# A graph network's first 112 nodes taken out of the count matrix and summed by gathers

## The chip, the cores and the metric

The kernel runs on one core of a Trainium2 chip. The core's engines each run their own stream of instructions and wait for each other through semaphores: TensorE (PE in the profile, its weight loads PEld), VectorE (DVE), ScalarE (ACT), GpSimd (POOL) and SyncE (SP), which only issues DMAs. ACT and POOL issue DMAs too. The metric is the time of one execution on the device, in microseconds (us).

## The reference

There are N = 2500 nodes with 256 features and E = 80000 directed edges, sorted by destination (about 32 edges a node). Cut to what matters:

```python
h = relu(layernorm(x))
xs = [h]
for W, b in ((W0, b0), (W1, b1), (W2, b2)):          # three layers
    xi, xj = h[dst], h[src]
    m = concatenate([xi, xj - xi], -1) @ W + b        # W is 512 x 256
    s = segment_sum(m, dst, N)                        # sum over the edges of each node
    h = relu(s / max(cnt, 1))                         # cnt: edges of each node
    xs.append(h)
out = x + concatenate(xs, -1) @ Wf + bf
```

Since the sum is linear, with W split into Wt (top half) and Wb, the sum for node n is cnt[n] * h[n] @ (Wt - Wb) + (sum over its edges of h[src] @ Wb) + cnt[n] * b. The middle term is a product with the count matrix A, where A[m, n] is the number of edges from node m to node n.

## The kernel before

**Layout.** Nodes stand in NT = 20 tiles of 128 (NP = 2560 rows). `hT` holds the features transposed, 256 features x NP nodes. `zh` and `zl` hold z = h @ Wb for all nodes, as a rounded part and the remainder, so that two fast matmuls (float32r) give nearly float32 accuracy. `acc` gathers the output, one tile of 128 nodes x 256 at a time. Row PAD of the last tile of `zh`, `zl` holds the bias, and row PAD of the count matrix holds `cnt`, so that the bias enters by the same product.

**Count matrix.** Destinations are taken in windows of W = 6 nodes: 417 windows, whose edges are fetched by indirect DMA (`get_edges`, L542), one window to a partition, in WG = 4 rounds of 128 windows, at most CAP = 256 edges each. `compare` (L755, VectorE) makes one-hot matrices of four windows, `counts` (L773, PE) multiplies them, `take_counts` (L782, ACT) writes the result to the tile `a`. Windows are put together in NG = 5 groups of columns: four of 84 windows (504 columns) and one of 81 (486 columns). A finished group is given its row of counts by `finish` (L800, on POOL) and stored to DRAM (`a_dram`), since only two groups fit in SBUF; layers 1 and 2 load three groups each (`load_a`, L806).

**A layer.** `layer` (L817) makes one group of columns: for each of the 20 node tiles and both halves of the features, one matmul with `zh` and one with `zl` as weights and the group of `a` as the moving operand (80 matmuls, L832), then four float32 matmuls with `wt` and `hT` (eight instructions on PE, L836), then a ReLU on ACT that overwrites the group's columns of `hT` (L839). Before a layer's groups, `nodes_split` (L708) makes `zh` and `zl` from `hT` tile by tile (L711, L720, L721). `final` (L731) adds a tile's product with its part of Wf to `acc` (L734, L736) before the tile of `hT` is overwritten.

**Order.** The stage before layer 0 follows a list written out by hand (L864): normalisation (N), transposes (T, R), products (Z, H, L for z, F, G for the output), edge search and the counting of group 0 (B, C, E). Layer 0 makes group g while the counts of group g + 1 are built between its matmuls; most of its instructions are recorded through a helper that keeps them in program order, so they all carry line L280. Layers 1 and 2 run the groups up or down, so that the two groups left in SBUF come first. In layer 1 `add_x` (L724) brings x and the last bias to `acc`: 20 DMAs on POOL's queue and 40 additions on POOL. After layer 2 the last 20 `final` calls store the output.

**Queues.** SP issues the loads of inputs and weights and the stores and loads of `a`; POOL issues the indirect DMAs and those of `add_x`. Each queue issues in order: an instruction that waits holds back all behind it.

Of the kernel before, what the change touches and what calls it, by code (L numbers as in the profile page):

```python
# [280 lines left out]
        return ordered  # L281


DONE = object()


def run(it):
    for _ in it:
        pass
# [22 lines left out]
def by_windows(ctx: ExitStack, tc: tile.TileContext, x, src, dst, Ws, bs, Wf, bf, out, missing):  # L312
# [13 lines left out]
    CH = 2  # L326
    S = 8
    CAP = CH * P
    NW = (N + W - 1) // W
    NV = NW * W  # L330
    WG = (NW + P - 1) // P
    NB = NT * W
    BW = 4
    TURN = 3
# [1 line left out]
    AHEAD = 4  # L336
    GWS = []
    while sum(GWS) < NW:
        GWS.append(min(84, NW - sum(GWS)))
    G = max(GWS) * W  # L340
    GS = 512
    NG = len(GWS)
    Q = NT // 2
    assert NT == 2 * Q
# [2 lines left out]
    MORE = 4 - R % 4  # L347
    HR = (R + MORE) // 2
    assert NP <= 4096 and HR <= 512
    assert E == P * R and NV <= NP and BW * NB <= 512 and G <= 512 and CAP <= 256  # L350
    assert E + P < 2 ** 24 and NV - (NT - 1) * P <= PAD < P and D == DC * P

    const = ctx.enter_context(tc.tile_pool(name="const", bufs=1))
    dram = ctx.enter_context(tc.tile_pool(name="wdram", bufs=1, space=DRAM))
# [32 lines left out]
    lim = const.tile([P, WG], F32, name="lim")  # L387

    const.tile([P, 24], F32, name="between")
    a_dram = [dram.tile([P, NT, G], F32, name=f"a_dram{g}") for g in range(NG)]  # L390

    apools = [ctx.enter_context(tc.tile_pool(name="apool0", bufs=1))]
# [40 lines left out]
    load_wt(0, SPo)  # L433

    lim_i = pp.tile([P, WG], I32, name="lim_i")
    POOLo.iota(lim_i, pattern=[[P * W, WG]], base=0, channel_multiplier=W)
    limr_i = pp.tile([P, WG * P], I32, name="limr_i")
    POOLo.iota(limr_i, pattern=[[W, WG * P]], base=0, channel_multiplier=0)
    row_i = pp.tile([P, MORE], I32, name="row_i")
    POOLo.iota(row_i, pattern=[[0, MORE]], base=-P, channel_multiplier=1)  # L440
    make_identity(nc, ident)
# [10 lines left out]
    load_b(1)  # L452
    DVE.memset(ones, 1.0)
    DVE.memset(ones_b, 1.0)
    DVE.memset(cnt[:, NV:], 0.0)
    POOL.tensor_copy(ident_b, ident)
    warm = pp.tile([P, 1], F32, name="warm")
    ACTo.activation(warm, ones, AF.Sqrt)
    idle = pp.tile([P, 512], BF16, name="idle")
# [94 lines left out]
    def key_parts(i):  # L554
# [3 lines left out]
        DVEo.tensor_scalar(away[:, i, :], ed, lim[:, i:i + 1], -1.0, op0=OP.subtract, op1=OP.max)  # L558
        parts[i] = [lo_i]

    def key_low(i):
        km = pw.tile([P, CAP], F32, name="km")
        ACTo.copy(km, parts[i][0])
        parts[i][0] = km

    def key_high(i):

        hi_i = edges[i][0]
        DVEo.tensor_scalar(hi_i, hi_i, ~(P - 1), 4, op0=OP.bitwise_and, op1=OP.logical_shift_right)
        kn = pw.tile([P, CAP], F32, name="kn")  # L570
        DVEo.scalar_tensor_tensor(kn, away[:, i, :], float(W), hi_i, op0=OP.min, op1=OP.add)
        parts[i].append(kn)
# [15 lines left out]
    def degrees(i):  # L588

        for q in range(W + 2):  # L590
            junk = hot.tile([P, CAP], BF16, name="junk2")
            ACTo.activation(junk, away[:, i, :], AF.Relu, bias=nc_[:, q:q + 1], accum_out=gsum[:, i, q:q + 1])
            yield
        DVEo.scalar_tensor_tensor(deg[:, i, :], gsum[:, i, 1:W + 1], -2.0, gsum[:, i, 0:W], op0=OP.mult, op1=OP.add)
        DVEo.tensor_add(deg[:, i, :], deg[:, i, :], gsum[:, i, 2:W + 2])
        DVEo.tensor_copy(deg_b[:, i, :], deg[:, i, :])
        yield
        yield
        yield
        yield  # L600
        for w0 in range(0, min(P, NW - i * P), P // 2):
            n = min(P // 2, NW - i * P - w0)
            pc = bank()
            for c in range(W):
                PEo.matmul(pc[:, :n * W].rearrange("p (w c) -> p w c", c=W)[:, :, c],
                          deg_b[:, i, c:c + 1].to_broadcast([P, P]), ident_b[:, w0:w0 + n], start=True, stop=True)
            ACTo.copy(cnt[:, (i * P + w0) * W:(i * P + w0 + n) * W], pc[:, :n * W])
            yield

    def shares():  # L610
        cnt_n = bank()
        for t in range(NT):
            PEo.matmul(cnt_n[:, t:t + 1], cnt[0:1, t * P:(t + 1) * P], ones_b, start=True, stop=True)
        found = hot.tile([P, 1], F32, name="found")
        DVEo.reduce_sum(found, deg.rearrange("p i c -> p (i c)"), axis=mybir.AxisListType.X)
        pf = bank()
        PEo.matmul(pf[0:1, 0:1], found, ones, start=True, stop=True)
        DVEo.tensor_scalar(missing, pf[0:1, 0:1], float(E), None, op0=OP.not_equal)
        yield
        some = hot.tile([P, NT], F32, name="some")  # L620
        DVEo.tensor_scalar(share, cnt_n[:, :NT], 1.0, None, op0=OP.max)
        DVEo.reciprocal(share, share)
        DVEo.tensor_scalar(some, cnt_n[:, :NT], 1.0, None, op0=OP.min)
        DVEo.tensor_mul(share, share, some)
        yield
# [95 lines left out]
            DVE.scalar_tensor_tensor(zl[:, t, :], pz[:, :D], sc, zh[:, t, :].bitcast(F32),  # L721
                                     op0=OP.mult, op1=OP.subtract)

    def add_x(t):  # L724
        n = P if t < NT - 1 else LAST
        xb = hot.tile([P, D], F32, name="zf")
        POOL.dma_start(xb[:n], x[t * P:t * P + n, :])
        POOL.tensor_add(xb[:n], xb[:n], bf_sb[:n])
        POOL.tensor_add(acc[:n, t, :], acc[:n, t, :], xb[:n])

    def final(l, t):  # L731
        po = bank()
# [7 lines left out]


    def group_of(g):
        return sum(GWS[:g]) * W, GWS[g] * W

    def touched(g):
        c0, n = group_of(g)
# [52 lines left out]

    def finish(g, a):  # L800
        c0, n = group_of(g)
        POOLo.tensor_copy(a[PAD:PAD + 1, NT - 1, :n], cnt[PAD:PAD + 1, c0:c0 + n])
        SP.dma_start(a_dram[g][:, :, :n], a[:, :, :n].bitcast(F32))
        yield

# [4 lines left out]
        return a  # L810

    def by_count(g):
        c0, n = group_of(g)
        for o in range(DC):
            DVEo.tensor_mul(hT[:, o, c0:c0 + n], hT[:, o, c0:c0 + n], cnt[:, c0:c0 + n])

    def layer(l, g, a, own, PE=PE, ACT=ACT):  # L817

# [27 lines left out]

    groups = [(0, 1), (1, 2), (2, 4), (4, 6), (6, 8), (8, Q)]
    a = new_a(0)
    acts = {
        "lim": limits, "first": find_first, "next": find_next, "pick": find_rows,  # L850
        "dstr": lambda: ACTo.copy(dst_r[:, MORE:], dst_i),
        "pk": lambda i: pick_half(i // 10, i % 10), "sg": lambda i: count_half(i // 10, i % 10),
        "se": lambda i: search(*((0, 1), (1, WG))[i]), "ge": get_edges,
        "ka": key_parts, "km": key_low, "kb": key_high, "kt": key_turn,
        "k1": lambda i: key_copy(i, 0), "k2": lambda i: key_copy(i, 1),
        "io": small_numbers, "ws": lambda: DVEo.tensor_sub(ws[0][0], ws[0][0], ws[0][1]),
        "st": stats, "rs": lambda g: spread(*groups[g]), "sq": lambda g: roots(*groups[g]),
        "sc": lambda g: scales(*groups[g]), "N": normalize, "T": turn, "R": take_turned,
        "Z": lambda q: product(q, ws[0][1]), "V": lambda q: with_b(), "H": split_high, "L": split_low,
        "F": lambda q: product(q, wfs[0]), "G": first_final,  # L860
        "B": compare, "C": counts, "E": lambda b: take_counts(b, a),
        "warm": keep_warm,
    }
# [3 lines left out]
        sc3 L0 sg21 N6 pk31 ka0 kb0 Z1 N5 st8 N7 G1 T6 rs5 sg10 sg31 km0 T5 se1 kt0 R6 H1 st2 F6 sq5 sc5 k10 k20  # L867
        rs2 Z6 ge1 L1 T7 B0 R5 R7 Z5 B1 C0 B2 ka1 G6 H6 N9 H5 C1 T9 F7 E0 ge2 kb1 R9 sq2 km1 E1 kt1 C2 B3 k21 Z9
        k11 N8 L6 B4 E2 L5 C3 B5 C4 T8 E3 E4 C5 V9 R8 E5 ge3 ka2 H9 sc2 Z7 H7 F8 G7 B6 N3 N2 ka3 km2 T2 R2 km3
        kb2 C6 T3 kb3 B7 L7 kt2 Z2 B8 B9 L9 E6 C7 k22 k12 kt3 H2 N4 E7 B10 k13 k23 Z8 L2 C8 T4 C9 E8 C10 H8 E9  # L870
        F9 B11 B12 C11 G8 E10 C12 R4 E12 E11 B13 F5 B14 C13 R3 B15 C14 E13 E14 L8 B16 Z3 G9 B17 C15 C16 H3 E15
        G5 B18 F3 C17 E16 C18 F4 E17 B19 C19 Z4 L3 G3 B20 E18 C20 B21 F2 E19 B22 E20 H4 L4 G4 B23 B24 G2 ws
    """

    def perform(order):
# [20 lines left out]

    held = None
    LATE = [NT] * 4
    extra = chain(degrees(0), finish(0, a), later_loads(), degrees(1))
    for g in range(NG):  # L900
        at = {}
        own = LATE
        if g + 1 < NG:
            a1 = new_a(g + 1)
            one = build(g + 1, a1)
            left = -(-len([b for b in windows if b[0] == g + 1]) // TURN)
            units = NT + DC * DC
            at = {(i + 1) * (units - 1) // left - 1 for i in range(left)}
            if g:
                own = [u + 1 - i for i, u in enumerate(sorted(at)[1:5])]  # L910
        else:
            extra = shares()
        for u, _ in enumerate(layer(0, g, a, own, PEo, ACTo)):
            if u in at:
                next(one)
            next(extra, None)
            if g == 0 and u % 2:
                next(extra, None)
            if g == 0 and u == NT // 2 + 3:
                by_count(0)  # L920
            if u == NT - 1 and g + 1 < NG:
                run(extra)
                by_count(g + 1)
        run(extra)
        if g + 1 < NG:
            run(finish(g + 1, a1))
            held, a = a, a1
        extra = chain(degrees(g + 2) if g + 2 < WG else ())
    DVEo.tensor_sub(ws[1][0], ws[1][0], ws[1][1])
    tiles = {NG - 1: a, NG - 2: held}  # L930
    for l in range(1, L):
# [1 line left out]
        if l % 2:  # L933
            groups.reverse()

        last = touched(groups[0])
        for t in [t for t in range(NT) if t not in last] + last:
            nodes_split(l, t)
        if l + 1 < L:
            load_b(l + 1)  # L940
            load_wb(l + 1)
# [2 lines left out]
        for j, g in enumerate(groups):  # L944
            for t in touched(g):
                if t not in finished:
                    finished.add(t)
                    final(l, t)
                    if l == 1:
                        add_x(t)  # L950
            if j == NG - 1:
                load_wf(l + 1)
            run(layer(l, g, tiles[g], LATE))
# [2 lines left out]
            if j + 2 < NG:  # L956
                del tiles[g]
                tiles[groups[j + 2]] = load_a(groups[j + 2])

    for t in [*range(NT - 3), NT - 1, NT - 3, NT - 2]:  # L960
        final(L, t)
# [38 lines left out]
```

## Time and profile before

| What | Value |
|---|---|
| Median of 3 runs | 517.1 us (517.03 to 517.1) |
| The profiled execution's own time | 517.24 us |
| Its span, first to last instruction | 515.4 us |
| Granted TensorE clock | 0.999 of full speed |
| Stage before layer 0 | to 62.3 us |
| Layer 0 (counts built inside) | 62.3 to 210.5 us |
| Layer 1 | 210.5 to 352.0 us |
| Layer 2 | 352.0 to 493.3 us |
| Last stage | 493.3 to 515.4 us |
| One group's load or store of `a` | 5040 KB, 17.2 to 17.3 us from issue to landing |

The stages are read from the chain that ended last: the work followed back from the last instruction, at each step to what released it. "Busy" is the time in which an engine had an instruction under way; matmuls overlap, so the cost of one is the distance from start to start, which is the length of a piece of the chain over the number of instructions in it. A float32 matmul is two instructions on PE.

### The profile page before, as it was taken

The numbers are of one execution on the slowest core, as the hardware profiler recorded it, in microseconds if no ns is written. First come the engines' busy times: TensorE is split into PE (matmuls) and PEld (weight loads), VectorE is DVE, ScalarE is ACT, GpSimd is POOL, SyncE is SP. The second block draws the span as 40 slices with busy tenths as digits, with TensorE's granted clock in tenths as the row PEclk, the third lists the DMA queues.
The fourth block names the chain that finished last, engine by engine and source line by source line (L and its number), as shares of the span: only waits on it lengthen the run. The fifth ranks groups of instructions, "written<-read, shape, count | busy, mean of one in ns | idle before, by whom it ended". The sixth has DMA issues, their size and how long they took to land.

```text
span 515.4 us, 6981 instructions
## 1 busy us (share of the span) xinstructions
PE 508.1 (99%) x2864; PEld 407.2 (79%) x2864; DVE 213.5 (41%) x455; ACT 134.1 (26%) x307; POOL 68.5 (13%) x103
## 2 busy tenths in 40 slices
PE   8999999999999999999999999999999999999996
PEld 4898888778778788788787878787887878787875
DVE  7989998889888840360101010103501010101033
ACT  5776666644534320330000000004300000000000
POOL 2680000000000000017241424200000000000000
PEclk9999999999999999999999999999999999999999
DMA  9110008950906428011576665100005565730023
GB/s 277 50 43 0 1 2 325 336 215 15 378 11 232 171 80 318 22 31 48 180 261 207 236 229 214 32 1 1 1 0 197 205 219 183 252 136 20 1 84 121
DMA packets 38111, 68.74 MB, mean 133 GB/s; under 512 B 1201, under 2 KB 37065, under 8 KB 38071
## 3 DMA queue, kind: packets, MB, share of 16 engines
q1 hardware_dynamic: 35798, 63.49, 34.8%
q0 software_dynamic: 1344, 3.61, 2.3%
q10 hardware_dynamic: 928, 1.11, 0.7%
q8 instruction: 24, 0.39, 0.3%
q14 instruction: 17, 0.13, 0.1%
HBM read 40.03 MB, written 28.18 MB: 132 GB/s over the span
## 4 chain that ended last, share of the span: by engine, by line
PE 90%; DVE 4%; DMA 3%; POOL 2%; issue 1%; SPq 0%; DVEq 0%
PE pa L832 35%; PE pa L280 21%; PE bank L734 10%; PE bank L280 8%; PE bank L711 7%; PE pa L836 7%; PE pz L280 2%; DMA acc<-in_x_dram 2%; POOL acc L280 1%; DVE one_m L280 1%; DVE st L280 1%; DMA es<-in_src_dram,start_i 1%; POOL ed L280 1%; DVE one_n L280 1%; POOL es L280 0%
## 5 line engine op out<-in xcount | busy, mean ns | idle before, releaser
L832 PE MATMUL pa<-a,zh 128*128 128x504 f32 (+1 forms) x400 | 156.4, 391 | 0.0
L832 PE MATMUL pa<-a,zl 128*128 128x504 f32 (+1 forms) x400 | 154.5, 386 | 0.0
L736 DVE SCALAR_TENSOR_TENSOR acc<-bank,share,acc 128x256 f32<-128x256 f32 x60 | 29.0, 484 | 213.6 <-PE bank L734 213.5
L832 PEld LDWEIGHTS pa<-a,zh 128*128 128x128 f32 x400 | 75.2, 188 | 14.9
L832 PEld LDWEIGHTS pa<-a,zl 128*128 128x128 f32 x400 | 75.1, 188 | 14.8
L280 PE MATMUL pa<-a,zh 128*128 128x504 f32 (+1 forms) x200 | 84.0, 420 | 0.0
L280 DVE TENSOR_TENSOR one_m<-iota_m,key_m 128x1024 bf16<-128x1024 bf16 (+1 forms) x105 | 72.1, 687 | 15.2 <-PE bank L280 15.1
L280 PE MATMUL pa<-a,zl 128*128 128x504 f32 (+1 forms) x200 | 77.7, 389 | 0.0
L839 ACT ACTIVATE hT<-pa 128x1008 f32<-128x1008 f32 (+1 forms) x10 | 10.1, 1005 | 238.8 <-PE pa L836 238.8
L280 ACT CAST a<-bank 128x480 fp32r<-128x480 f32 (+1 forms) x105 | 52.9, 565 | 68.5 <-PE bank L280 65.9
L280 DVE TENSOR_TENSOR one_n<-iota_n,key_n 128x960 bf16<-128x960 bf16 (+1 forms) x105 | 69.7, 664 | 0.0
L734 PE MATMUL bank<-wf,hT 128*128 128x256 f32 x240 | 53.6, 379 | 0.0
L734 PEld LDWEIGHTS bank<-wf,hT 128*128 128x128 f32 x240 | 45.6, 190 | 9.8 <-issue 4.1
L280 PEld LDWEIGHTS <-one_m 128*128 128x128 bf16 x834 | 45.5, 98 | 9.8 <-issue 7.0
L280 PE MATMUL bank<-one_n,one_m 128*128 128x120 bf16 x834 | 51.4, 217 | 0.3
L280 PEld LDWEIGHTS pa<-a,zh 128*128 128x128 f32 x200 | 37.8, 189 | 10.3 <-issue 2.6
L280 PEld LDWEIGHTS pa<-a,zl 128*128 128x128 f32 x200 | 37.7, 189 | 8.9 <-issue 2.6
L721 DVE SCALAR_TENSOR_TENSOR zl<-bank,share,zh 128x256 fp32r<-128x256 f32 x38 | 18.4, 484 | 56.0 <-ACT zh L720 55.9
L836 PE MATMUL pa<-hT,wt 128*128 128x504 f32 (+1 forms) x80 | 35.2, 582 | 0.0
L711 PE MATMUL bank<-wb,hT 128*128 128x256 f32 x160 | 34.9, 379 | 0.0
L711 PEld LDWEIGHTS bank<-wb,hT 128*128 128x128 f32 x160 | 30.4, 190 | 4.9 <-issue 0.9
L836 PEld LDWEIGHTS pa<-hT,wt 128*128 128x128 f32 x80 | 15.1, 189 | 14.5 <-issue 13.8
(113 smaller groups left out, 333.2 us busy)
## 6 DMA issues: line engine op xcount, KB each, us to landing
a<-a_dram SPq DMA_DIRECT2D x5, 5040.0 KB, 17.3
a_dram<-a SPq DMA_DIRECT2D x4, 5040.0 KB, 17.2
a_dram<-a SPq DMA_DIRECT2D x1, 4860.0 KB, 17.1
a<-a_dram SPq DMA_DIRECT2D x1, 4860.0 KB, 15.1
zf<-in_x_dram POOLq DMA_DIRECT2D x19, 128.0 KB, 4.2
out_dram<-acc SPq DMA_DIRECT2D x19, 128.0 KB, 1.7
wf<-in_L_gnn_Wf_dram SPq DMA_DIRECT2D x4, 256.0 KB, 9.0
acc<-in_x_dram SPq DMA_DIRECT2D x1, 896.0 KB, 10.1
```

What stands on the lines that cost most here:

```text
L280: return self.tc.keep_in_program_order(call(*args, **kwargs))
L711: PE.matmul(pz[:, :D], hT[:, c, t * P:(t + 1) * P], ws[l][1][:, c, :], start=(c == 0), stop=(c == DC - 1))
L721: DVE.scalar_tensor_tensor(zl[:, t, :], pz[:, :D], sc, zh[:, t, :].bitcast(F32), op0=OP.mult, op1=OP.subtract)
L734: PE.matmul(po[:, :D], hT[:, c, t * P:(t + 1) * P], wfs[l][:, c, :], start=(c == 0), stop=(c == DC - 1))
L736: DVE.scalar_tensor_tensor(acc[:, t, :], po[:, :D], share[:, t:t + 1], acc[:, t, :], op0=OP.mult, op1=OP.add)
L832: PE.matmul(pa[:, o, :n], z[:, i, o * P:(o + 1) * P], a[:, i, :n], start=(i == 0 and z is zh), stop=(z is zl and last[o] == (kind, i, o)))
L836: PE.matmul(pa[:, o, :n], ws[l][0][:, c, o * P:(o + 1) * P], hT[:, c, c0:c0 + n], start=False, stop=(last[o] == (kind, i, o)))
L839: ACT.activation(hT[:, :, c0:c0 + n], pa[:, :, :n], AF.Relu)
```

## The change

The first FEW = 112 nodes no longer have columns in the count matrix. The other 2388 are 398 windows of six, in four groups of 80 windows (480 columns) and one of 78 (468 columns). The last round of the edge search has 14 windows left over (IN_LAST); the 112 nodes take the partitions behind them, one node to a partition, with at most EDGES = 64 edges each. `few_edges` puts the source nodes of these edges in `who`, and a node of zeros (number NP - 1) where a node has fewer.

Each layer now also writes z to DRAM: `keep_nodes` stores `zh` from SP's queue and adds `zl` to it by an accumulating DMA from POOL's queue. `gather` then issues 64 indirect DMAs from POOL: number e fetches for each partition the row of z that its e-th edge names. They go in turn into four slots of `sums`; the first four write, the other 60 add. `add_sums` adds the four slots on VectorE, and `layer_few` makes the 112 columns of the new `hT`: four matmuls with `wt`, the bias by the last tile of `zh` and `zl` and the counts in `cnt_few`, and the sums by a matmul with a piece of the identity (`only`), which transposes them and drops the partitions that hold no node.

In the stage before layer 0 the stores (X) and accumulations (Y) are put in the list. In layers 1 and 2 tile 0, which holds the 112 nodes, is made last of the 20; `layer_few` comes after a layer's last group. `add_x` becomes five accumulating DMAs from POOL and four additions of the bias on VectorE, after layer 1's last group in program order. The row of counts in `finish` is written by ACT. Rows of `a` are as long as a group (GS = 480, before 512), so a full group is one contiguous run in a partition.

```diff
-    NW = (N + W - 1) // W
+    FEW = 112
+    EDGES = 64
+    SUMS = 4
+    NW = (N - FEW) // W
...
+    IN_LAST = NW - (WG - 1) * P
+    NONE = NP - 1
...
-        GWS.append(min(84, NW - sum(GWS)))
+        GWS.append(min(80, NW - sum(GWS)))
     G = max(GWS) * W
-    GS = 512
+    GS = 480
...
+    def few_edges():
+        es, ed = edges[WG - 1]
+        own = pp.tile([P, EDGES], I32, name="own")
+        POOLo.tensor_scalar(who, es[:, :EDGES], -NONE, None, op0=OP.add)
+        POOLo.tensor_scalar(own, away[:, WG - 1, :EDGES], 0.0, None, op0=OP.is_equal)
+        POOLo.tensor_tensor(who, who, own, op=OP.mult)
+        POOLo.tensor_scalar(who, who, NONE, None, op0=OP.add)
...
-    def add_x(t):
-        n = P if t < NT - 1 else LAST
-        xb = hot.tile([P, D], F32, name="zf")
-        POOL.dma_start(xb[:n], x[t * P:t * P + n, :])
-        POOL.tensor_add(xb[:n], xb[:n], bf_sb[:n])
-        POOL.tensor_add(acc[:n, t, :], acc[:n, t, :], xb[:n])
+    def add_x():
+        for t in range(0, NT, 5):
+            n = min(t + 5, NT - 1) - t
+            POOLo.dma_start(acc[:, t:t + n, :], xr[:, t:t + n, :], accum_op=OP.add)
+        POOLo.dma_start(acc[:LAST, NT - 1, :], x[(NT - 1) * P:N, :], accum_op=OP.add)
+        for t in range(0, NT, 5):
+            DVE.tensor_add(acc[:, t:t + 5, :], acc[:, t:t + 5, :], bf_sb.unsqueeze(1).to_broadcast([P, 5, D]))
...
-        POOLo.tensor_copy(a[PAD:PAD + 1, NT - 1, :n], cnt[PAD:PAD + 1, c0:c0 + n])
+        ACTo.copy(a[PAD:PAD + 1, NT - 1, :n], cnt[PAD:PAD + 1, c0:c0 + n])
...
+    def keep_nodes(l, a, b):
+        to = z_dram[l][a * P:b * P, :].rearrange("(k p) d -> p k d", p=P)
+        SPo.dma_start(to, zh[:, a:b, :].bitcast(F32))
+        yield
+        POOLo.dma_start(to, zl[:, a:b, :].bitcast(F32), accum_op=OP.add)
+
+    def gather(l, n):
+        for e in range(n):
+            POOLo.indirect_dma_start(
+                out=sums[:, e % SUMS, :], out_offset=None, in_=z_dram[l][:, :],
+                in_offset=bass.IndirectOffsetOnAxis(ap=who[:, e:e + 1], axis=0),
+                **({"compute_op": OP.add} if e >= SUMS else {}))
+
+    def add_sums():
+        DVEo.tensor_add(sums[:, 0:2, :], sums[:, 0:2, :], sums[:, 2:4, :])
+        DVEo.tensor_add(sums[:, 0, :], sums[:, 0, :], sums[:, 1, :])
+
+    def layer_few(l):
+        pa = ps_agg.tile([P, DC, 512], F32, name="pa")
+        for o in range(DC):
+            for c in range(DC):
+                PEo.matmul(pa[:, o, :FEW], ws[l][0][:, c, o * P:(o + 1) * P], hT[:, c, :FEW],
+                           start=(c == 0), stop=False)
+            for z in (zh, zl):
+                PEo.matmul(pa[:, o, :FEW], z[:, NT - 1, o * P:(o + 1) * P], cnt_few, start=False, stop=False)
+            PEo.matmul(pa[:, o, :FEW], sums[:, 0, o * P:(o + 1) * P], only, start=False, stop=True)
+        ACTo.activation(hT[:, :, :FEW], pa[:, :, :FEW], AF.Relu)
...
+    gather(0, EDGES)
     extra = chain(degrees(0), finish(0, a), later_loads(), degrees(1))
...
+    add_sums()
+    layer_few(0)
     DVEo.tensor_sub(ws[1][0], ws[1][0], ws[1][1])
...
-        last = touched(groups[0])
-        for t in [t for t in range(NT) if t not in last] + last:
-            nodes_split(l, t)
+        last = [t for t in touched(groups[0]) if t]
+        for ts in by_runs([t for t in range(1, NT) if t not in last] + last + [0]):
+            for t in ts:
+                nodes_split(l, t)
+            run(keep_nodes(l, ts[0], ts[-1] + 1))
+        gather(l, EDGES)
...
+        if l == 1:
+            add_x()
+        add_sums()
+        layer_few(l)
```

`by_runs` cuts the list of tiles into runs of neighbours, at most five long; in layers 1 and 2 it gives three runs of five, one of four, and tile 0 alone.

## The prediction

> **What bounds the kernel now.** I read the page's busy table first, then the chain that ended last in order of time. The page:
>
> ```profile
> span 515.4 us, 6981 instructions
> PE 508.1 (99%) x2864; PEld 407.2 (79%) x2864; DVE 213.5 (41%) x455; ACT 134.1 (26%) x307; POOL 68.5 (13%) x103
> ```
>
> The chain (start, length, engine, tile, line; pieces of one kind merged) in layer 1's beginning and layer 2's end:
>
> ```profile
> 210.52 17.27 PE bank L711 x80
> 227.79 4.32 PE bank L734 x20
> ...
> 447.72 18.15 PE pa L832 x80
> 465.87 3.38 PE pa L836 x8
> 469.25 3.45 PE bank L734 x16
> 472.70 17.34 PE pa L832 x80
> 490.05 3.26 PE pa L836 x8
> 493.31 17.28 PE bank L734 x80
> ```
>
> From 47.6 us on the chain is TensorE (PE) alone, piece against piece: every instruction taken from PE shortens the run, every wait put on PE lengthens it. 80 count-matrix matmuls of 504 columns take 18.15 us (226.9 ns each), 80 of 486 columns 17.34 us (216.8 ns).
>
> POOL is idle through layer 2 and most of layer 1; the change moves work there. What that work costs is read from the groups by shape (busy, mean ns of one, idle before):
>
> ```profile
> L280 POOL DMA_INDIRECT ed<-in_dst_dram,start_i x4 | 4.2, 1058 | 10.0 <-DVE off L280 8.2 <-DVE start_i L280 1.5 <-issue 0.3
> L280 POOL DMA_INDIRECT es<-in_src_dram,start_i x4 | 3.8, 954 | 1.2 <-issue 1.2
> ```
>
> from the DMA issues, with the median time to landing:
>
> ```profile
> zf<-in_x_dram POOLq DMA_DIRECT2D x19, 128.0 KB, 4.2
> ...
> ed<-in_dst_dram,start_i POOLq DMA_INDIRECT x4, 3.1
> es<-in_src_dram,start_i POOLq DMA_INDIRECT x4, 2.8
> ```
>
> and from the answer on the tile `zf`:
>
> ```profile
> DMA to landing us min/median/max: 2.0/3.8/5.7
> ```
>
> `ed` and `es` are gathers of the new size (128 rows of 1 KB), without the addition: 0.95 to 1.06 us on POOL plus about 0.31 us before the next one, landed after 2.8 to 3.1 us. `zf`, the same bytes beside the big count-matrix loads, shows what DMA load does: up to 5.7 us. No accumulating DMA stands in this trace.
>
> **What the Trainium skill says.** (1) "DMA: Bandwidth & Descriptors", section "Anatomy of one DMA — SWDGE (gpsimd) path": about 2.0 us of a POOL-issued DMA is fixed, mostly the write's receipt, and waits are kept by the issuing engine, not by the DMA engines. The trace agrees: 2.8 us to land 128 KB. (2) The same page, "Rules for kernel authors": an accumulating DMA must wait for the earlier one on the same bytes. Hence each gather waits for the fourth before it (built order: POOL's gather e waits for the landing of e-4). (3) "SBUF — State Buffer", "Who interferes with whom": VectorE's 2-port modes lock descriptor generation out, `tensor_tensor` has none. Agrees: compares beside the indirect DMAs at 26.7 to 33.6 us keep 0.65 to 0.70 us, but for one of 0.98. (4) "TensorE: Matmul & The Clock Gate", Part 1: a PE gap over about 3.4 us may halve the clock. Not seen here (granted clock 0.999).
>
> **The change part by part.**
>
> *Count-matrix matmuls.* Groups go from 4x504 + 486 to 4x480 + 468 columns. From the two forms the slope is (226.9-216.8)/18 = 0.56 ns a column: 13.5 ns off 504, 10.1 off 486. In proportion it would be 10.8 and 8.0 ns. Per layer 320 and 80 of them: 5.1 or 4.1 us; I take 4.6. The `wt` matmuls: 422.5 to 407.5 ns for 18 columns, 0.83 ns a column: 32 x 20 + 8 x 15 ns = 0.8. Together **5.4 us a layer (4.9 to 5.9), 16.2 in three**.
>
> *Counting.* 417 windows become 398: 38 fewer counting matmuls; 24 take 1.28 us, so 53 ns each: **2.0 us**, 0.4 of it before layer 0. VectorE loses five compare pairs (1.2 us each). It is not the bound in layer 0 (busy 26.6 of 31.1 us at 98.9 to 130 us); after, some 25.3 of 28.9.
>
> *`layer_few`.* Per layer 8 float32 `hT` passes, 4 `z` matmuls, 4 passes on `sums`: 16 instructions of 112 columns. Nearest rows: float32 transposes of 128 columns start 0.11 us apart; a float32 weight load of 128 columns takes 0.19. I take 0.15: **2.4 us a layer (1.8 to 3.0), 7.2 in all**. It stands on PE's path between the last group and the next layer's products. Tile 0 is made last there, so its ReLU is hidden by 19 other tiles (16 us); in the last stage tile 0 is first: a wait for an ACT of 224 columns (256 take 0.47 us) plus semaphores, **0.7 us**.
>
> *Preamble.* New iotas and memsets on POOL lie in its 8.25 us idle before the first `ed`; `few_edges` and the `z` stores come after POOL's last normalisation at 38.4 us, when only the gathers stand behind them. On SP they precede the first `a` store, needed by nobody until layer 1. The pad-row copy moves from POOL to ACT (0.8 us, five times; ACT is half idle in layer 0). All zero on the path; without the cover, 3 us at most.
>
> *The gathers*, 64 a layer, wholly on POOL. Time per gather T is the larger of the issue (0.98 + 0.31 = 1.3 us) and a quarter of the landing time, since four are in flight. The addition is unknown: below, it costs nothing beside a plain gather (T 1.3); above, POOL's part doubles with a third party to each row, 2 x 0.98 + 0.31 = 2.3 us (T 2.3). I take landing 4 to 5.5 us, thus T 1.3 to 1.4. Most late entries read one and the same row; `bf_sb` (one row to 128 partitions) shows 46 ns packets, so I price that at nothing. Limits, from the shortened path:
> - Layer 0: start about 66 us, path ends at 210.5 - 5.0 = 205.5: T up to 2.1.
> - Layer 1: products end near 223; the last tile's store (about 2.5 us, and held on SP behind the load of the next `wb`, which waits for all products), then its accumulate (1 + 3 us), so start at about 232; last group ends near 342. Behind the gathers on POOL stand the five DMAs of `add_x`; on VectorE the four additions of `bf` (512 columns take 0.68 us, so 1.4 each) stand ahead of `add_sums`, and that ahead of PE's `only` matmuls. Those five: 0.55 us (the 128-row DMA) to 2.75 us (five times that) of issue each, landing 3 to 4 us, then 2.5 us on VectorE: 10 to 20 us after the last gather. T up to (343 - 15 - 232)/64 = 1.5.
> - Layer 2: start 370, end 480: T up to 1.65.
> With T = 1.3 to 1.4 all is hidden.
>
> *Removed:* `add_x`'s 40 POOL additions were off the path: nothing.
>
> Sum: 16.2 + 2.0 - 7.2 - 0.7 = 10.3 us less. Span 515.4 - 10.3 = 505.1; the profiled execution took 517.24, 1.8 us around the span, and lies 0.14 us over the median of 517.1, so 506.8. For the chance of a short wait at layer 1's end I write 507.5.
>
> **The rivals.**
>
> *A, gathers too slow; slower than before.* PE waits at `only`. At T = 2.0 layer 1 is ready at 232 + 128 + 15 = 375 against 343: 32 us; layer 2 needs 133 us where it has 111: 21 us. 507 + 53 = 560. It turns into a loss where 64(T - 1.5) passes 10 us, T = 1.65. For it: nothing in the trace bounds the addition, and SBUF must be read before it is written. Against it: plain gathers land in 2.8 us, so landing may double to 5.6 before T reaches 1.4. T = 2.3, the upper bound, delays all three layers (12, 51 and 41 us): about 610.
>
> *B, only layer 1's end is late.* T between 1.45 and 1.65, or slow `add_x` DMAs: 1 to 10 us of PE wait, 508 to 517.
>
> *C, the gathers delay the count-matrix loads.* A load takes 17.3 us and has about 24. A gather of 32 packets of 158 ns on 16 engines takes 0.32 us of every 1.3, a quarter: 17.3/0.75 = 23, barely in time. If the addition doubles a packet, about 2 us on each of six loads: 510 to 522. Against it: rows of `a` become contiguous (2016-byte packets now, 23 bytes/ns; 4096-byte ones run at 26).
>
> *D, matmuls do not get shorter* since the 188 ns weight load bounds them: `wt` and counting save 2.4 + 2.0, `layer_few` and the last stage cost 7.9: 520.6. Against it: the 486 form is already 10 ns shorter.
>
> **How the numbers follow.** Hidden gathers 0.50 (own range 503.5 to 510.5); B 0.15; A 0.25; C 0.07; D 0.03. Faster by over 0.2% (516.1), about what a measurement here can tell from no change: all of the first, nearly all of B less a few hundredths, a little of C and A: 0.66; within 0.2%: 0.04; slower: 0.30. The range runs from 503.5 to 535: under it 0.06, over it 0.14, the far part of A.
>
> **What would show it.** Spacing of 480-column matmuls 213 to 216 ns; POOL's gathers 1.3 us apart, done 10 us or more before each last group ends; no PE idle before the `only` matmuls. Wrong if those wait on VectorE, and VectorE on gathers (A) or on `acc<-in_x` (B), or if `pa<-a` waits for an `a` load (C).

## The result

The changed kernel takes 647.12 us (median of 4 runs, 646.8 to 647.63) where the kernel before takes 517.07: a ratio of 1.2517, 95% interval 1.2495 to 1.2539. The forecast was 507.5 us, range 503.5 to 535. It is wrong in direction and in size, and the time is 37 us beyond the 610 that rival A gave for its worst case.

The page of the changed kernel, beginning with the busy table; then TensorE's and POOL's busy tenths and the granted clock, in 40 slices of the span:

```profile
span 645.5 us, 7186 instructions
PE 506.7 (78%) x2875; PEld 416.4 (65%) x2875; DVE 216.6 (34%) x458; ACT 135.9 (21%) x312; POOL 355.8 (55%) x264
...
PE   8999999999996029999999950007999999990066
...
POOL 3871653848376741255364888840253648788800
PEclk9999999999999559999999985557999999995569
```

TensorE's busy time is about what it was (506.7 us, before 508.1), but there are three holes in it, at slices 14 to 15, 24 to 27 and 37 to 38. They are the ends of the three layers. POOL is busy before each hole and idle in part of it. The list of waits names the holes (engine, tile, line, what it waited for: us in total, times, longest):

```profile
PE pa L280 <- DVE sums L280: 131.0, 3, 59.5
DVE sums L280 <- DMA sums<-z_dram,who: 108.7, 2, 55.9
POOL sums L280 <- DMA sums<-z_dram,who: 94.2, 24, 11.1
DVE acc L787 <- DMA acc<-in_x_dram: 73.3, 4, 68.0
```

The first line is the whole loss. TensorE waits three times, 131 us in all, for VectorE's `add_sums`, just before the matmuls with `only`; 645.5 less 131.0 is 514.5, about the span of before. VectorE waits twice for gathers and once (layer 1) behind the `bf` additions, which wait for `add_x`. The size of the third line was not foreseen: POOL itself stood still 24 times for a gather's landing, up to 11.1 us each.

The groups by shape give a gather's price (busy, mean ns | idle before it), and the answer on the tile `sums` the landing:

```profile
L280 POOL DMA_INDIRECT sums<-z_dram,who x192 | 299.9, 1562 | 161.3 <-DMA sums<-z_dram,who 94.2 <-issue 56.8 <-DMA z_dram<-zl 10.4
```

```profile
DMA to landing us min/median/max: 2.8/4.6/16.7
```

An accumulating gather holds POOL for 1.54 us (median), where the plain ones of before took 0.95 to 1.06; with the 0.30 us between two, they are 1.85 us apart at best. And some land late, after up to 16.7 us (the trace gives a landing for 48 of the 192). The chain that ended last, in layer 1 (start, length, what), shows both prices, and then the tail:

```profile
281.23 15.25 DMA sums<-z_dram,who
296.48 0.26 issue
296.74 1.53 POOL sums L280
298.27 0.30 issue
298.58 1.54 POOL sums L280
...
304.10 16.16 DMA sums<-z_dram,who
...
419.49 2.83 POOL acc L280 x2
422.31 14.80 DMA acc<-in_x_dram
...
438.61 0.70 DVE sums L280
...
439.81 2.48 PE pa L280 x10
```

The table by stretch of layer 1 (length, then busy us of each engine with the number of instructions, the clock, the share of the DMA engines, GB/s) puts a number on it:

```profile
276.00:345.00 69.00, 69.00 (x297) 55.73 (x296) 5.92 (x12) 2.89 (x3) 34.81 (x24) 1.00 0.83 259
345.00:418.00 73.00, 35.31 (x151) 27.75 (x150) 1.94 (x4) 1.94 (x2) 60.16 (x40) 0.75 0.52 73
```

While `a` is being loaded, POOL gets 24 gathers out in 69 us; afterwards 40 in 73 us. The loads slow the gathers, 2.9 us each instead of 1.8. The records of single DMA packets say how: a load of `a` in the changed kernel goes in packets of 38,400 bytes, one partition's 20 rows of 480 in one run, at 1.43 us each (median, 276 to 345 us). In the kernel before they were 2,016 bytes at 0.088 us. An accumulating gather is 128 packets of 1,024 bytes at 0.10 us; spread evenly, eight of these fall to each of the 16 DMA engines.

### The profile page after: what moved, and what is told of

The parts are those of the page before. It is cut to its first block, busy times and chain, and to the rows that moved or that the text cites. A ratio compares the mean times of both kernels' runs of the same rounds, so it can differ in the third digit from the quotient of the medians.

```text
span 645.5 us, 7186 instructions
## 1 busy us (share of the span) xinstructions
PE 506.7 (78%) x2875; PEld 416.4 (65%) x2875; DVE 216.6 (34%) x458; ACT 135.9 (21%) x312; POOL 355.8 (55%) x264
## 4 chain that ended last, share of the span: by engine, by line
POOL 23%; DMA 21%; issue 7%; PE 6%; DVE 0%; ACT 0%; POOLq 0%; DVEq 0%; ACTq 0%
POOL sums L280 23%; DMA sums<-z_dram,who 16%; PE bank L792 3%; PE bank L767 3%; DMA acc<-in_x_dram 2%; DMA z_dram<-zl 1%; DMA z_dram<-zh 1%; PE pa L280 1%; POOL acc L280 0%; DVE sums L280 0%; POOL z_dram L280 0%; DVE acc L794 0%; ACT zh L776 0%; ACT hT L280 0%; POOLq L280 0%
## 5 line engine op out<-in xcount | busy, mean ns | idle before, releaser
L280 POOL DMA_INDIRECT sums<-z_dram,who x192 | 299.9, 1562 | 161.3 <-DMA sums<-z_dram,who 94.2
L921 PE MATMUL pa<-a,zh 128*128 128x480 f32 (+1 forms) x400 | 154.2, 386 | 0.0
L921 PE MATMUL pa<-a,zl 128*128 128x480 f32 (+1 forms) x400 | 152.0, 380 | 0.0
L280 PE MATMUL pa<-only,sums 128*128 128x112 f32 x12 | 4.5, 477 | 131.0 <-DVE sums L280 131.0
L280 PE MATMUL pa<-a,zh 128*128 128x480 f32 (+1 forms) x200 | 81.6, 408 | 0.0
L280 PE MATMUL pa<-a,zl 128*128 128x480 f32 (+1 forms) x200 | 75.8, 379 | 0.0
L280 DVE TENSOR_TENSOR one_m<-iota_m,key_m 128x1024 bf16<-128x1024 bf16 x100 | 68.7, 687 | 17.0 <-PE bank L280 16.8
L280 POOL DMA_DIRECT2D z_dram<-zl x15 | 20.3, 1462 | 83.3 <-DMA z_dram<-zh 68.8
L280 DVE TENSOR_TENSOR one_n<-iota_n,key_n 128x960 bf16<-128x960 bf16 x100 | 65.2, 652 | 0.0
L280 ACT CAST a<-bank 128x480 fp32r<-128x480 f32 x100 | 50.6, 565 | 59.5 <-PE bank L280 58.4
L928 ACT ACTIVATE hT<-pa 128x960 f32<-128x960 f32 (+1 forms) x10 | 9.7, 967 | 232.5 <-PE pa L925 232.5
L792 PEld LDWEIGHTS bank<-wf,hT 128*128 128x128 f32 x240 | 46.7, 195 | 10.3 <-issue 3.4
L280 DVE TENSOR_TENSOR sums<-sums 128x512 f32<-128x512 f32 (+1 forms) x6 | 3.4, 558 | 108.8 <-DMA sums<-z_dram,who 108.7
```

Source lines behind the costliest of these rows:

```text
L280: return self.tc.keep_in_program_order(call(*args, **kwargs))
L792: PE.matmul(po[:, :D], hT[:, c, t * P:(t + 1) * P], wfs[l][:, c, :], start=(c == 0), stop=(c == DC - 1))
L921: PE.matmul(pa[:, o, :n], z[:, i, o * P:(o + 1) * P], a[:, i, :n], start=(i == 0 and z is zh), stop=(z is zl and last[o] == (kind, i, o)))
L928: ACT.activation(hT[:, :, c0:c0 + n], pa[:, :, :n], AF.Relu)
```

## The experiments

All times are to be read against the kernel before, 516.9 to 517.2 us in every set of runs. "Wait" is TensorE's wait for `add_sums`, all layers together.

| Kernel | Edges | Addition | Row of `a` | `add_x` | Wait, us | Time, us |
|---|---|---|---|---|---|---|
| changed | 64 | yes | 480 | layer 1's end | 131.0 | 647.1 |
| e1 | 64 | yes | 488 | layer 1's end | 74.6 | 592.3 |
| e2 | 64 | no | 480 | layer 1's end | 64.4 | 581.2 |
| e3 | 4 | none | 480 | layer 1's end | 1.4 | 510.3 |
| e4 | 48 | yes | 488 | layer 1's end | 5.9 | 515.7 |
| e5 | 64 | no | 488 | layer 1's end | 22.2 | 543.1 |
| e6 | 48 | yes | 488 | layer 0, not in order | none | 581.5 |
| e7 | 48 | yes | 480 | layer 1's end | 42.5 | 558.6 |
| e9 | 48 | yes | 488 | layer 0, in order | none | 508.1 |
| e10 | 64 | yes | 488 | layer 0, in order | 58.5 | 574.4 |
| e11 | 64, no row of zeros | no | 488 | layer 1's end | 4.0 | 532.1 |
| e12 | 64, no row of zeros | no | 488 | layer 0, in order | none | 534.4 |

e2, e3, e5, e11 and e12 leave out part of the sums and serve for timing alone. e8 is the kernel before with other groups, at the end.

**e1: rows of 488.** With rows longer than a group, a partition's part of a group is no longer one run.

```diff
-    GS = 480
+    GS = 488
```

> Only the row length of the tile a is changed, 480 to 488 numbers, so that a load or store of a no longer moves one run of 38,400 bytes per partition but runs of 1,920. Theory 'long packets' (a gather's packets queue on each DMA engine behind 38,400-byte packets of 1.43 us each): no gather lands after more than about 6 us, the gathers keep 1.85 us apart also during loads, 64 take 118 us; the wait before `only` vanishes in layer 0, falls to about 35 us in layer 1 and 19 us in layer 2, time about 570 us. Rival 'bytes' (the load takes the DMA engines whatever its packets are): landings up to 17 us remain, time 640 to 650 us.

592.25 us (one run). Loads and stores of `a` now go in packets of 1,920 bytes (0.08 us). POOL's waits and the landing:

```profile
POOL sums L280 <- DMA sums<-z_dram,who: 40.5, 44, 2.7
...
DMA to landing us min/median/max: 2.7/6.9/10.8
```

POOL waits at most 2.7 us for a landing, and in layers 1 and 2 the gathers are 1.85 us apart (median), mean 1.88, loads or not; before this edit the means were 2.25 and 2.16. Thus the packets, not the bytes, starved the gathers: 55 us of the loss. The Trainium skill, "DMA: Bandwidth & Descriptors", section "Queues, rings and completion order", says that a DMA engine takes turns between queues, a whole packet at a time. The packet records of the changed kernel agree. From 309.8 to 317.0 us, in the middle of a load, every 1.45 us (about the length of one long packet) 15 or 16 gather packets start and as many long ones, one of each for each of 16 engines. At that pace few gathers get through a load: in layer 1's three loads 48, 115 and 192 gather packets start between the first long packet and the last, at 128 to a gather.

The changed kernel also holds a comparison of its own. Its group of 468 columns leaves the end of each row of 480 free, so it is moved in packets of 1,872 bytes. Beside its load in layer 2 POOL stands still for landings for 1.1 us in all, beside the two others for 9.8 and 10.8.

The short packets have a price that this edit's time doesn't show: the load now gives up turns too. Its landings, where the trace has them, are 23.0 and 26.8 us, against 17.3 and 17.5 in the changed kernel.

The theory missed twice. Gathers land after up to 10.8 us, where it said 6. And in layer 0 they are 2.2 us apart, so TensorE waits 18.6 us there, where it said none; hence 592 and not 570. In layer 0 VectorE's compares run beside the gathers: 15 gathers beside which VectorE did nothing held POOL for 1.54 us, 45 that compares overlapped by over 0.3 us for 1.70 (medians). No run changes this alone, so it is a correlation. The prediction's point (3) had looked at the compares' time, not at POOL's.

**e2: no addition.** The same kernel as the changed one, but every gather writes, so the sums are left out.

```diff
-                in_offset=bass.IndirectOffsetOnAxis(ap=who[:, e:e + 1], axis=0),
-                **({"compute_op": OP.add} if e >= SUMS else {}))
+                in_offset=bass.IndirectOffsetOnAxis(ap=who[:, e:e + 1], axis=0))
```

> The gathers write instead of add (the 112 nodes' sums are not formed); everything else stays, the long packets too. Theory 'the addition is what POOL pays': 0.95 us on POOL and 1.3 us from gather to gather outside loads, against 1.54 and 1.85. If the addition also splits a gather into 128 packets of 1 KB where a plain one has 32 of 4 KB, each engine has 2 packets of it and not 8, and landings during loads stay near 5 us: waits of about 5 us in all, about 520 us. Rival: during loads only about five gathers pass in 17 us as now, and the time is about 560 us.

581.23 us (one run). POOL's part falls to 0.95 us (median), so the addition does cost 0.6 us of issue each. But POOL waits for landings instead:

```profile
POOL sums L280 <- DMA sums<-z_dram,who: 142.1, 88, 7.8
```

Neither cause alone is the loss. The theory's 520 fails, and the rival's 560 is too low as well: the long packets remain, and the last quarter of a layer's gathers has packets of 0.6 to 0.8 us, of which e5 and e11 show more.

**e5: both.** Rows of 488 and no addition.

> Gathers without the addition and rows of a 488 long; the additions of the sums are left out of the computation. Theory (the addition's longer issue on POOL and the long packets are the two causes, and together all of it): gathers about 1.3 to 1.4 us apart throughout, no waits before the matmuls with only but for layer 1's end, 508 to 516 us. Rival (64 gathers a layer are too many beside the loads of a, whatever their kind): over 1.6 us apart while a load runs, waits in all three layers, 540 us or more.

543.14 us (one run): the rival's figure. The gathers' median distance is 1.43 and 1.48 us in layers 1 and 2, but the mean is 1.64. Two things hold it there. Landings take 6.3 us (median), and a quarter of that is 1.58. And towards the end of a layer the packets get slow: by eighths of layer 1's gathers their mean time is 166 to 243 ns in the first four, and 591 and 664 in the last two, and the last eighth is 1.63 us apart with no load under way. The late entries are nearly all the row of zeros: a node has 19 to 47 edges, 31.2 in the mean, so half of the 64 x 112 entries name one and the same row. With gathers this slow beside it, a load of `a` is late too (the third of layer 1 lands after 33.2 us), which is rival C; the list of waits of e5:

```profile
PE pa L280 <- DVE sums L280: 22.2, 3, 17.7
PE pa L920 <- DMA a<-a_dram: 5.3, 2, 2.7
```

TensorE waits for `a` once in each of layers 1 and 2, 5.3 us together.

**e11: no row that all read.** As e5, and past a node's last edge the gathers read the sources that follow in the list.

```diff
-        own = pp.tile([P, EDGES], I32, name="own")
-        POOLo.tensor_scalar(who, es[:, :EDGES], -NONE, None, op0=OP.add)
...
-        POOLo.tensor_scalar(who, who, NONE, None, op0=OP.add)
+        POOLo.tensor_copy(who, es[:, :EDGES])
```

> As the kernel with plain gathers and rows of 488, and few_edges no longer replaces what lies past a node's last edge by the row of zeros: the gathers read the next nodes' sources there, so rows all over z. Left out of the computation: the additions of the sums and the mask of a node's own edges. Theory (late gathers were slowed by reading one and the same row: packets of 650 to 780 ns where early ones take 165 to 220, and 1.6 to 1.8 us apart with no load under way): packets of 165 to 230 ns to the end, late gathers 1.3 to 1.45 us apart outside of loads, layer 1's last one near 335 us, a wait of 5 to 10 us there because of add_x, none in layers 0 and 2: 515 to 522 us. Rival (the late packets are slow for another reason): unchanged, 541 to 545 us.

The gathers did as the theory said: packets of about 165 to 235 ns to the end (means by eighths), the last eighth 1.25 us apart in layer 1, layer 1's last gather at 333.7 us, and one wait for `add_sums`, 4.0 us in layer 1. So the one row was the cause of the slow late packets. But the time is 532.14 us (one run), over the theory's 522. TensorE loses 5 to 7 us more in each layer, near the end of the gathers. Its matmuls start up to 2 us apart while it waits for nothing that the profile shows, and then the granted clock is 0.5 for 3 to 7 us:

```profile
332.30 0.37 PE L916 MATMUL pa<-a,zl 128*128 128x480 f32 x1
333.72 0.37 PE L916 MATMUL pa<-a,zh 128*128 128x480 f32 x1 [1.04 <-issue]
335.82 0.56 PE L916 MATMUL pa<-a,zl 128*128 128x480 f32 x1 [1.73 <-issue]
```

**e12: the same with `add_x` in layer 0** (the edit of e9 below).

> The same, with add_x issued after layer 0's gathers and bf added in order at the start of layer 1; the additions of the sums and the mask of a node's own edges are left out of the computation. Theory (short issue, short packets on the loads, no row read by all, no add_x behind layer 1's gathers: then 64 gathers a layer are hidden as the forecast had it): no wait of 1 us before the matmuls with only, 506 to 511 us. Rival (64 gathers cannot be hidden beside the loads of a): waits of 3 us or more in a layer, 513 us or more.

No wait for `add_sums` at all, as the theory said, and yet 534.41 us (one run): TensorE has the same holes, one of over 10 us in layer 0 at 124 us, where gathers run mostly 1.25 us apart and no load or store of `a` does. The order of time there ("remote": released by something the profile doesn't name):

```profile
124.20 0.38 PE L280 MATMUL pa<-a,zl 128*128 128x480 f32 x1 [0.48 <-issue]
130.02 0.56 ACT L280 CAST a<-bank 128x480 fp32r<-128x480 f32 x1 [6.69 <-remote]
134.31 0.56 ACT L280 CAST a<-bank 128x480 fp32r<-128x480 f32 x1 [3.73 <-remote]
134.92 0.77 PE L280 MATMUL pa<-a,zh 128*128 128x480 f32 x1 [10.34 <-issue]
```

By their order, the two ACT copies wait for counting matmuls that ended at 121.98 and 123.00 us. They start when TensorE's semaphore is next updated, at 129.99 and 134.29, so the news of finished work came 8 and 11 us late. Over all kernels such a copy, where ACT stood idle before it, starts 0.04 us after its matmul (median), and at most 1.3 us after it in every kernel but two: up to 5.5 us in e11 and 11.3 in e12. So in these two kernels TensorE's semaphore updates fall behind, and TensorE stops as well. What holds them up is not settled. In e11 and e12 gathers follow each other 1.25 us apart for up to 17 and 16 in a row, in e2 and e5, which have no such holes, for at most 11 and 9; that is all the trace offers. Each of the two is a single execution.

**e3: four gathers a layer.** `gather(0, SUMS)` and `gather(l, SUMS)` in place of EDGES; most of each sum is left out.

> Only the first 4 of 64 gathers per layer are issued (the sums are incomplete). No wait before `only` except perhaps for add_x; the rest of the change stands. My sum of the prediction says 505 to 507 us; from the trace after, where the count-matrix matmuls of 480 columns start 220 ns apart instead of 214, I expect 511 to 513 us. If the wait in layer 1 comes from add_x or the z stores and not from the gathers, a wait of over 5 us stays there.

510.29 us (509.54 to 512.99), ratio 0.9876 (0.9841 to 0.991), a little under the 511 that I expected at least. So the rest of the change is worth 7 us and `add_x` is part of what it still costs: in layer 1, TensorE waits 1.4 us behind it even now.

**e4 and e7: 48 edges.** `EDGES = 48` holds every node here (at most 47 edges). e7 is this alone, e4 with rows of 488.

> EDGES 48 alone, rows of a 480 long as in the changed kernel. Theory (the long packets cost as much per layer with 48 gathers, since they stall POOL for 8 to 13 us at each load whatever the number of gathers): no wait in layer 0, some 20 to 25 us in layer 1, 5 to 9 in layer 2: 538 to 546 us. Rival (64 edges were the only fault): 514 to 518 us, as with rows of 488.

> 48 gathers per layer instead of 64 (no node of the 112 has more than 47 edges), and rows of a of 488 numbers. With both theories (1.85 us a gather, no starving): 89 us of gathers, layer 0 done by 160 us, layer 1 at 35 + 89 + 18 = 142 us after its first product against 139: a wait of 3 us, layer 2 none: about 514 to 518 us. If long packets are not the cause, three loads a layer cost 24 us more of gathers: layer 1 waits 27 us, layer 2 about 8, about 545 us.

e7: 558.59 us (one run), waits of 6.6, 29.1 and 6.8 us: each store or load of 480 columns sets the gathers back by 7 to 11 us against their 1.85, with 48 of them as with 64, and layers 0 and 1 wait more than I gave them. e4: 515.67 us (514.54 to 517.14), ratio 0.9974 (0.9964 to 0.9984), a little faster than before. The chain of e4 at layer 1's end names what is left:

```profile
327.22 1.54 POOL sums L280
328.76 2.83 POOL acc L280 x2
331.59 14.35 DMA acc<-in_x_dram
...
348.64 2.48 PE pa L280 x10
```

The last gather ends at 328.8 us, in time for 342.8 where TensorE begins to wait; `add_x` and the sums behind it take 20 us more.

**e6 and e9: `add_x` early.** The five DMAs go behind layer 0's gathers. In e6 the four `bf` additions are called at the start of layer 1, as before through plain `DVE`; e9 is e6 with these through `DVEo`, the helper that keeps program order.

```diff
     gather(0, EDGES)
+    load_x()
...
         gather(l, EDGES)
+        if l == 1:
+            add_bf()
...
-        if l == 1:
-            add_x()
```

> EDGES 48, rows of a 488 long, and in addition the five DMAs of add_x are issued after layer 0's gathers and the four additions of bf come at the start of layer 1. Theory (what is left of the loss in the kernel with 48 edges is add_x behind layer 1's gathers: the 6 us that PE waits before layer 1's matmuls with only, and some 1 us of lower clock after it): no wait there, 508 to 510 us, ratio to the kernel before 0.982 to 0.986. Rival (the gathers themselves end too late in layer 1): the wait stays at 3 us or more, 512 to 515 us.

e6: 581.52 us, ratio 1.126 (1.1242 to 1.1279). My edit did something else than I meant, and the waits say what:

```profile
DVE acc L789 <- DMA acc<-in_x_dram: 71.9, 1, 71.9
PE bank L280 <- DVE one_n L280: 70.6, 2, 70.4
```

Instructions not recorded in program order are placed by the planner, the part of the framework that orders each engine's instructions. It put a `bf` addition among layer 0's compares on VectorE, 72 us before x had landed, and TensorE's counting waited for the compares. Layers 1 and 2 had no wait.

> As the kernel with add_x issued early (EDGES 48, rows of 488), but the four additions of bf are recorded in program order, so that on VectorE they stand at the start of layer 1 and no longer among layer 0's compares, where they held VectorE for 72 us until x had landed. Theory (layers 1 and 2 of that run had no wait before the matmuls with only; its 70.6 us gap in layer 0 is all that stood against it): 579.8 less 70.6, so a span near 508 and 508 to 511 us. Rival (layer 1's gathers end too late once layer 0 is not stretched): a wait of 3 us or more in layer 1, 512 to 515 us.

e9: 508.08 us (507.98 to 508.21), ratio 0.9824 (0.981 to 0.9837): 1.8% less than the kernel before, and the least of all here, with nothing of the computation left out. It relies on no node among the first 112 having over 48 edges; the kernel's own limit `most` sends other inputs to the general path. The page, and layer 1's end in the chain:

```profile
span 506.4 us, 7136 instructions
PE 499.0 (99%) x2875; PEld 410.7 (81%) x2875; DVE 216.1 (43%) x458; ACT 136.0 (27%) x312; POOL 284.7 (56%) x216
```

```profile
322.04 17.45 PE pa L923 x80
339.49 3.22 PE pa L927 x8
342.71 1.77 PE pa L280 x16
344.48 5.63 PE bank L767 x26
```

TensorE goes from the last group into `layer_few` and on to the next layer's products without a gap.

**e10: e9 with 64 edges.**

> The same with EDGES 64: add_x early and in order, rows of 488, 64 accumulating gathers a layer. Theory (gathers bound by POOL's issue, 1.54 + 0.31 us apart, 64 of them taking 120 us): no add_x in layer 1's tail, so waits of about 10 to 16 us in layer 0, 20 in layer 1 and 20 in layer 2, 560 to 570 us. Rival (the tail of add_x made most of layer 1's wait): under 10 us in layer 1, 545 to 555 us.

574.4 us (one run), waits of 18 to 20 us in every layer. These are the theory's waits, but for 18.3 us in layer 0 where it had 10 to 16, and a time a little over its 570. So e9 needs the smaller number of gathers, and `add_x` was worth the 18 us between e1 and e10.

**e8: the kernel before with other group sizes,** 84, 84, 84, 80 and 85 windows, rows of 512.

> The kernel before with groups of 84, 84, 84, 80 and 85 windows, so that matmuls of 504, 480 and 510 columns all run with rows 512 long. Time about as before, 516 to 519 us. What it tells is the distance of the 480-column matmuls from start to start: 213 to 216 ns if the change's rows of 480 are what kept them at 219 to 220; 219 to 220 if 480 columns cost that anywhere.

518.06 us (one run). From a group's first count-matrix matmul to its `wt` matmuls the 80 take 18.84 us at 510 columns, 18.34 at 504, 17.53 and 17.61 at 480; the kernel before has 17.79 and 17.53 at 486, in layers 1 and 2. So 480 columns cost 219 to 220 ns here too, the second of the two outcomes named, and are hardly shorter than 486. The changed kernel has 17.76 at 480. Its rows of 480 aren't the whole reason: e7, with the same rows and 48 edges, has 17.65, and kernels with rows of 488 have 17.62 (e1, e9). What the last tenth of a microsecond depends on stays open.

## Why the prediction was wrong

Along one line of edits the spans go 645.5 (changed), 590.5 (short packets), 572.7 (`add_x` early), 506.4 (48 gathers). The forecast's span with hidden gathers was 505.1. Its sum for TensorE's work comes within 1.3 us of e9, in part by luck: the matmuls gave less, other terms cost less. What it said of the gathers fails in each term.

- **T, the issue: the step that failed first.** "The issue (0.98 + 0.31 = 1.3 us)" is 1.54 + 0.30 = 1.85. I had bounded the addition between 1.3 and 2.3 and took the lower end, with the argument that plain gathers land early. That speaks of landing, not of POOL's own time, and the working's own limits for layers 1 and 2 (1.5 and 1.65) left no room for the middle of the bracket. By these limits 1.85 is too long for layers 1 and 2, and e10, with short packets and `add_x` out of the way, still waits 18 to 20 us a layer.
- **T, the landing.** "I take landing 4 to 5.5 us" was read from `zf`, beside loads in packets of 2,016 bytes. The change itself made those packets 38,400 bytes long. I had noticed that "rows of `a` become contiguous", and set it down in rival C as a help to the loads. Beside the gathers it was one (17.3 and 17.5 us, with short packets 23.0 and 26.8), and the gathers paid: up to 16.7 us.
- **"I price that at nothing"** (one row read by all): false for plain gathers, where packets go from about 0.17 to over 0.65 us and T from 1.25 to 1.63 (e11, e5). In the accumulating kernel it doesn't show in the distance: in layers 1 and 2 early and late gathers without a load are 1.85 us apart.
- **Layer 1's start.** 26.5 us after the products begin became 35 (241.0 to 276.1): the last `zh` store lands after 6.8 us, where I had 2.5, and the first gather starts 8.0 us after the `zl` accumulate behind it is issued, where I had 4.
- **`add_x`'s tail.** "10 to 20 us after the last gather": the last gather starts at 417.9 and `add_sums` at 438.6, 20.7 us, just past the far end of the range. The mis-sized part is the landing of the last DMA, 14.8 us where I had 3 to 4. The tail takes the room that e4 needed; moving it saves 18 us at 64 gathers and 7.6 at 48.
- **Rival A** is what happened: the wait stands before `only`, in all three layers. Its price was for T = 2.3 in all layers; T came to 2.57, 2.25 and 2.16 (means), layer 1 began late, and the tail was at its worst. Its chance of 0.25 was small for a term with a bracket of 1.3 to 2.3 and a limit of 1.5. **Rival B**, a wait at layer 1's end alone, is what e4 has left: 5.9 us.
- **Rival C** did not happen in the changed kernel: no matmul waited for a load. It appears only in e5, at 5.3 us. Its sum of 23 us for a load that has about 24 is close to what the loads with short packets take, so there is little to spare. **Rival D** did not happen either: the matmuls did get shorter.
- **Count-matrix matmuls:** 4.6 us a layer became 4 x 0.58 + 0.29 = 2.6 (in e9 4 x 0.72 + 0.34 = 3.2). The slope came from two forms, 504 and 486 columns, the latter from layer 2 alone (17.53 us for 80; 17.79 in layer 1); e8 shows that it doesn't continue to 480. The `wt` matmuls saved the 0.8 us as worked out.
- **`layer_few`:** 2.4 us a layer; where nothing waits it takes 1.77 (e9). **The last stage's wait:** 0.7 forecast; in e9 the step there is 0.67 us longer than in layers 0 and 1. **Layer 0's end** was forecast 5.0 us earlier than before; the products of layer 1 begin 5.2 us earlier in e9. In e9 the matmuls gave 4.2 us less than the sum had, `layer_few` cost 1.9 less, and about 1 us more came out of layer 0 (the remainder, not traced further): 9.0 us off the span, where the sum said 10.3.
- **The clock.** The Trainium skill, "TensorE: Matmul & The Clock Gate", Part 1, was cited for a drop after a long gap. It is there: in the changed kernel the granted clock falls to 0.5 2 to 4 us into a hole, and stays there until 4 to 6 us after TensorE starts again. The next 80 products take 17.9 and 18.1 us in place of 17.3. The forecast's sum gave a wait no such after-effect.

## What to carry to other kernels

Before work is put on an idle engine, give the new operation a range of prices and find the longest price that still hides; if that limit lies inside the range, a wait is as much to be expected as a gain. Look at what a change does to the length of contiguous runs: here runs of 38,400 bytes made each turn on a DMA engine 1.43 us long, and the small packets of the other queue waited for it. And what is queued behind the work that is just hidden, as `add_x` here, needs a place of its own.

## What had not been expected of the hardware

- An accumulating gather of 128 rows of 1 KB holds POOL for 1.54 us, a plain one for 0.95; the first goes in 128 packets of 1,024 bytes, the second in 32 of 4,096.
- A DMA from SP whose partitions are single runs of 38,400 bytes is moved in packets of that length, 1.43 us each. Gathers on another queue then land after up to 16.7 us instead of 10.8 at most (e1). The load lands after 17.3 and 17.5 us beside them, in packets of 1,920 bytes after 23.0 and 26.8 (e1). With few or no gathers in the kernel a load of that size takes much the same either way: 15.0 and 15.6 us in long packets (e3), 15.9 in short ones (e8).
- Plain gathers in which most rows are the same one have packets three to four times as long as those of scattered rows.
- Two kernels with long rows of plain gathers 1.25 us apart showed TensorE's semaphore updates up to 11 us late, and stalls of TensorE, 1 to 10 us long, that no wait in the profile explains (e11, e12). The cause stays open.
